# A two-layer relational graph network: 46 groups of edges of the second layer take their rows from on-chip memory instead of gathering them

## The chip, the cores and the metric

The kernel runs on one core of a Trainium2 chip. A core has five engines with queues of their own, each worked off in order: PE (TensorE, matrix products, with the weight loads counted apart as PEld), DVE (VectorE), ACT (ScalarE), POOL (GpSimd, which here issues the indirect gathers) and SP (SyncE, which here issues plain transfers). Engines wait for one another by semaphores. The metric is device time in microseconds of one execution; the kernel before took 4645.08 us (median of three runs, 4639.48 to 4657.33).

## The reference

There are 12500 nodes with 128 features each, 200000 edges sorted by target node, and 8 relations; source and relation of an edge are random. Each of two layers computes, for every node, the sum over relations of the mean of the messages that arrive by that relation, plus a root product and a bias; then a ReLU and the layer's input are added. At the end comes a layer norm over the features of the input plus the second layer's output.

```
W      = einsum('rb,bio->rio', comp, basis)
xw     = einsum('ni,rio->nro', x, W)
msgs   = xw[src, et]
seg    = dst * N_REL + et
summed = segment_sum(msgs, seg)
cnt    = segment_sum(ones, seg)
mean   = summed / maximum(cnt, 1)
agg    = mean.reshape(N_NODES, N_REL, HIDDEN).sum(axis=1)
h_new  = relu(agg + x @ root + bias);   h = h_new + h
...
out    = layernorm(x + h)
```

## The kernel before

Edges are cut into 1563 tiles of 128, and eight tiles form an octet (Q = 8, NQ = 196 octets; an octet has 1024 edges, the targets of which are some 64 neighbouring nodes). Targets are worked up in blocks of 128 nodes (98 of them), so an octet adds to one block, or to two.

Layer 1 gathers one row of x per edge, sums by node and relation with one-hot products (L1215), multiplies by the relation weights (L1247) and places the result in the block (L1278). As each block of its result is finished, `table` (L1346) multiplies it with all eight relation weights and writes the products to `y_d`, a table in HBM with a row for each pair of node and relation. The layer's result stays on chip as `hT`, features down the partitions and nodes along the columns.

Layer 2 gathers one finished row of `y_d` per edge (L678), so it has no relation products left. For octet q, the main loop puts into the queues: the gathers of octet q + 5; `slot_sums(q)`, eight products of 32 slots each that sum the gathered rows by target (L1442), and ACT's copy of the result `ys` (L628); `place_sums(q - 1)`, which puts the slots of the octet before at their nodes in the block's accumulator (L1467), with the root product where a block opens (L1471); the one-hot matrices of octet q + 2 on DVE (`slot_hots`: eight of 128x32 at L1091, one of 128x256 at L1094); and every second octet the closing of a block (L1299, L1303, L1323) and `open_block`, an ACT copy of a block of `hT`. After eight blocks a norm follows, with transposes on PE (L1585) and L1593 to L1613 on DVE. At its end an octet has `keep_on` (L1483): 12 products of 128x384 whose result nobody reads.

The rows of gathers lie in a ring of seven octet tiles; the gather of octet q + 7 waits until PE has read that of octet q. PSUM is used as fixed banks: `s` (two, the block accumulators in layer 2), `pt`, `ct`, `y` and two `po`; the slot sums of all octets and the norm's transposes share one `po`.

The order of work is written out by hand: each call appends to a list per engine, and `plan` turns the list into queues with semaphore waits. `plan.mark` names points at which an engine signals; with `plan.lazy` a wait is rounded up to the next such point.

In the list of functions below, the layer-1 loop and the layer-2 loop stand one after another; `later` is a list of small checks, of which one is done per octet.

Of the kernel before, what the change touches and what calls it, by code (L numbers as in the profile page):

```python
# [429 lines left out]
def ordered_path(  # L430
# [60 lines left out]
    BURST = 12  # L491
    DONE = NT - 4
    FULL = NQ - 4
    assert D == P and R * K == P and B == BF + 1 and 1 < TL and LAST < P and BF % 4 == 0 and Q == G and N % 2 == 0
    assert FULL == NQ - 4
# [61 lines left out]

    comp_sb = keep([P, L * R * NB], F32, "comp_sb")
# [38 lines left out]
    fails = keep([P, B + 4], F32, "fails")  # L597
# [54 lines left out]
    def gather(l, q):  # L652
        if q >= NQ:
            return
# [410 lines left out]
    def check_all():  # L1065
        pt, pc = pt_b
        pb = pt.rearrange("p b t -> p (b t)")
        pe(lambda: nc.tensor.matmul(pb[0:1, :B + 4], ones, fails, start=True, stop=True),
           ["ones"] + [("fails", b) for b in range(B + 4)], [pc])
        vec(lambda: nc.vector.tensor_reduce(nb_f, pb[0:1, :B + 4], axis=AX.X, op=ALU.max), [pc], ["nb_f"])  # L1070
        vec(lambda: nc.vector.tensor_copy(bad, nb_f), ["nb_f"], ["bad"])
# [27 lines left out]
    def onehot(l, q, g=None):  # L1099

        if l == 1 and q < FULL:
# [7 lines left out]
        if q >= NQ and (g is None or g < 0):  # L1109
            return  # L1110
# [264 lines left out]

    sT_all = [t.rearrange("p r g k -> p (r g k)") for t in sT_r.tiles]
    yr_all = [t.rearrange("p r d -> p (r d)") for t in yr_r.tiles]
    homes = {"idx": idx.bitcast(F32), "kr": kr, "sT0": sT_all[0], "sT1": sT_all[1], "yr0": yr_all[0], "yr1": yr_all[1],
# [14 lines left out]

    dm2_t = [home("sT0", Q * 2 * K, "dm2", i) for i in range(3)]
# [6 lines left out]
    dms2 = {}  # L1401
    hb_b = [(t, ("hb", i)) for i, t in enumerate((id_k, id_r, jmp.bitcast(F32)))]
    old.update({("hb", i): ["id_k", "id_r", "jmp"] for i in range(3)})
# [9 lines left out]
    hb = {}  # L1413
    misc = po_b[1]

    def open_block(k):
        n = rows_of(k)
        t, c = hb_b[k % 3]
        copy(t[:, :n], hT[:, k * P:k * P + n], [("h", k)], new(c))
        plan.mark("ACT")  # L1420
        hb[k] = t, c

# [10 lines left out]

    def slot_sums(q):
        t, c = rows_g.pop((1, q))
        d, dc = dms2.pop(q)
        b, bc = misc
        m0 = b[:, 3, :]

        def emit():  # L1440
            for i in range(Q):
                last = nc.tensor.matmul(m0[i // 2 * 2 * K:(i // 2 + 1) * 2 * K, :], d[:, i, :], t[:, i, :],  # L1442
                                        start=i % 2 == 0, stop=i % 2 == 1)
            return last

        pe(emit, [c + (0,), c + (1,), dc], [bc, ("done", 1)])
        plan.mark("PE")
        o, oc = ys[q] = ys_r.take()
        copy(o, m0, [bc], [oc])
        plan.mark("ACT")  # L1450

    def place_sums(q, k, opens, last):
# [5 lines left out]
        m = P  # L1458
# [17 lines left out]

    def keep_on():
        f = y_full[0]
        rhs = id_h[:, None, :].to_broadcast([P, 3, P])

        def emit():
            for _ in range(BURST):
                last = nc.tensor.matmul(f[:, :3, :], id_h, rhs, start=True, stop=True)  # L1483
            return last

        pe(emit, ["id_h"], [y_full[1]])
# [200 lines left out]
    def checks():  # L1687
        weights(1, (pt_b, pt_b))
        yield
        for b in range(B):  # L1690
            yield from check_edges(b)
        yield from check_span()
        yield from check_place()
        yield from fix_list()

# [19 lines left out]
    def end():  # L1715
        for k, step in ending:
            step()
            if k >= 0:
                tables.extend(table(k))
        ending.clear()  # L1720
# [8 lines left out]
    for o in range(NG - 3):  # L1729
# [11 lines left out]
        if parts is None:  # L1741
            run(later, 1)
# [22 lines left out]
        for i in range(2):  # L1765
            if turned_to:
                here = pt_b
                a, b = turned_to.pop(0)
            elif tables and o >= TABLE and (i == 0 or len(tables) > 6 or o > NG - 16):
                here = (pt_b, ct_b)[i]  # L1770
                a, b = tables.pop(0)(here)
            else:
                break
            while copies and here is not ct_b:
                copies.pop(0)(vcopy)
            a()
            if b is not None:
                copies.append(b)
        plan.mark("PE")
# [66 lines left out]
    for q in range(2):  # L1846
        onehot(1, q)
    open_block(0)
# [4 lines left out]
    for q in range(NQ):  # L1853
# [26 lines left out]
        if q == 0:  # L1880
            check_all()
        late = q - 1
        if q < FULL:
# [33 lines left out]
        if q < FULL:  # L1917
            keep_on()
# [67 lines left out]
```

## Time and profile before

| | |
|---|---|
| median of three runs | 4645.08 us (4639.48 to 4657.33) |
| profiled execution | 4616.74 us, span 4614.8 us |
| PE busy | 2424.3 us, 53% (weight loads 1713.5 us beside it) |
| DVE busy | 1386.0 us, 30% |
| ACT busy | 465.8 us, 10% |
| POOL busy | 2953.5 us, 64%, of which 1476.4 us in layer 1's gathers and 1475.0 us in layer 2's |
| mean granted clock of PE | 0.723 |
| DMA | 284.99 MB, mean 62 GB/s |

The profiled execution is 0.6% under the median of the runs. A row of the list of groups gives line, engine, operation, output and input, the count, the busy time and the mean of one in ns, and behind the bar the time in which the engine stood idle just before them, with what ended it. "issue" means that nothing the profile shows was waited for, "remote" that the releaser isn't in the records. Matrix products in float32 appear as two rows each, so eight of them are x16. The share of busy time is a mean over both layers; the prediction looks at layer 2 by itself, which lies between 2300 and 4600 us.

### The profile page before, as it was taken

To read this page: it belongs to the slowest core of one execution; us is meant where nothing else is said; L and a number is where in the kernel's file an instruction comes from. 1 tells how busy PE (TensorE), PEld (TensorE's weight loads), DVE (VectorE), ACT (ScalarE), POOL (GpSimd) and SP (SyncE) were. 2 spreads that over 40 slices of the span, in tenths; PEclk is the share of its full clock that TensorE was granted. 3 is DMA by queue.
4 is the path that set the end of the run, shared out by engine and by line. 5 is a ranking of instruction groups with operands and counts; after the bars stand their busy time and mean duration, and the time that the engine had idled before them with its cause. 6 is when DMAs were issued, how large, how long until landed. Compare 5 with 4: busy or idle time off the path is not lost.

```text
span 4614.8 us, 38428 instructions
## 1 busy us (share of the span) xinstructions
PE 2424.3 (53%) x14055; PEld 1713.5 (37%) x14055; DVE 1386.0 (30%) x4891; ACT 465.8 (10%) x1141; POOL 2953.5 (64%) x3135
## 2 busy tenths in 40 slices
PE   2666666555666566666644444444444444444445
PEld 1555554444555455555521222222222222222223
DVE  2544333333333233233312222222222222222223
ACT  0111112121211111111200000000000000000000
POOL 5666666666666666666556666666666666666664
PEclk9878777878777777777866666666666666666667
DMA  3111122223222222222221111112211212122121
GB/s 100 45 50 46 45 63 86 86 90 93 86 69 73 73 70 73 63 74 68 74 74 45 46 55 47 55 46 56 56 46 55 55 47 56 46 55 55 47 55 45
DMA packets 129830, 284.99 MB, mean 62 GB/s; under 512 B 54019, under 2 KB 61773, under 8 KB 129637
## 3 DMA queue, kind: packets, MB, share of 16 engines
q0 software_dynamic: 100064, 205.13, 17.1%
q10 hardware_dynamic: 16971, 52.05, 2.9%
q1 hardware_dynamic: 12602, 25.31, 1.6%
q8 instruction: 112, 1.84, 0.2%
q14 instruction: 81, 0.66, 0.0%
HBM read 223.63 MB, written 58.65 MB: 61 GB/s over the span
## 4 chain that ended last, share of the span: by engine, by line
another core or an unknown queue 41%; PE 32%; issue 20%; ACT 5%; DVE 2%; POOL 0%; DMA 0%; SPq 0%; ACTq 0%; POOLq 0%; DVEq 0%
PE y L1247 8%; PE y L1483 7%; PE s L1215 5%; PE po L1442 3%; ACT sT L628 2%; PE s L1467 2%; PE pt L1346 2%; PE po L1278 1%; ACT ys L628 1%; ACT y_row L628 1%; PE ct L1346 1%; DVE dm L1122 1%; PE po L1280 0%; PE s L1471 0%
## 5 line engine op out<-in xcount | busy, mean ns | idle before, releaser
L678 POOL DMA_INDIRECT rows<-in_x_dram,idx x1563 | 1476.4, 945 | 841.5 <-issue 438.7
L678 POOL DMA_INDIRECT rows<-y_d,idy x1563 | 1475.0, 944 | 768.9 <-issue 447.6
L1247 PE MATMUL y<-w_sb,sT 128*128 128x128 f32 x3136 | 544.9, 345 | 533.3 <-ACT ys L628 236.4
L1483 PE MATMUL y<-id_h 128*128 128x384 f16 x2304 | 598.3, 398 | 342.9 <-issue 335.2
L1247 PEld LDWEIGHTS y<-w_sb,sT 128*128 128x128 f32 x3136 | 512.0, 255 | 558.1 <-ACT ys L628 245.2
L1122 DVE TENSOR_SCALAR dm<-cols,kr,w 128x128 f32<-128x128 f16 x1563 | 526.1, 402 | 493.4 <-remote 232.4
L1091 DVE TENSOR_SCALAR sT<-cols,kr,w 128x32 f32<-128x32 f16 x1536 | 352.8, 302 | 724.7 <-remote 543.4
L1442 PE MATMUL po<-rows,sT 128*32 128x128 f32 x3072 | 173.5, 354 | 712.1 <-ACT ys L628 437.4
L1215 PEld LDWEIGHTS s<-dm,rows 128*128 128x128 f32 x3126 | 434.5, 217 | 175.3 <-ACT sT L628 106.3
L1483 PEld LDWEIGHTS y<-id_h 128*128 128x128 f16 x2304 | 259.7, 114 | 643.2 <-issue 563.8
L1215 PE MATMUL s<-dm,rows 128*128 128x128 f32 x3126 | 451.2, 303 | 81.3 <-ACT sT L628 61.7
L1442 PEld LDWEIGHTS po<-rows,sT 128*32 128x32 f32 x3072 | 102.2, 136 | 799.8 <-ACT ys L628 463.5
L628 ACT ACTIVATE sT<-s 128x512 f32<-128x512 f32 x391 | 212.4, 596 | 804.5 <-remote 543.6
L628 ACT ACTIVATE ys<-po 128x128 f32<-128x128 f32 x192 | 53.2, 277 | 2111.9 <-remote 1871.6
L1299 DVE TENSOR_TENSOR po<-po,carry 128x128 f32<-128x128 f32 x98 | 29.2, 298 | 663.1 <-remote 406.8
L1299 DVE TENSOR_TENSOR s<-s,carry 128x128 f32<-128x128 f32 x97 | 28.9, 298 | 616.4 <-remote 387.7
L1346 PE MATMUL pt<-w_sb,arena 128*128 128x512 f32 x258 | 156.3, 678 | 48.5 <-issue 41.2
L1467 PE MATMUL s<-pl,ys 128*128 128x256 f32 x288 | 139.6, 572 | 14.3 <-issue 14.2
L1278 PE MATMUL po<-pl,ys 128*128 128x256 f32 x392 | 138.9, 438 | 15.1 <-DVE pl L1130 6.5
L628 ACT ACTIVATE y_row<-pt 128x512 f32<-128x512 f32 x131 | 78.4, 598 | 659.2 <-remote 451.3
L1585 PE MATMUL po<-ident,wide 128*128 128x128 f32 x96 | 23.5, 388 | 193.6 <-ACT ys L628 153.3
L871 PE MATMUL ct<-arena,id_h 128*128 128x512 f16 (+1 forms) x188 | 75.5, 422 | 85.9 <-issue 44.5
(214 smaller groups left out, 1565.0 us busy)
## 6 DMA issues: line engine op xcount, KB each, us to landing
y_d<-y_row ACTq DMA_DIRECT2D x96, 512.0 KB
rows<-in_x_dram,idx POOLq DMA_INDIRECT x1563
rows<-y_d,idy POOLq DMA_INDIRECT x1563
x_g<-in_x_dram SPq DMA_DIRECT2D x24, 512.0 KB
out_dram<-x_g SPq DMA_DIRECT2D x12, 512.0 KB
arena<-in_L_gnn_basis_dram SPq DMA_DIRECT2D x2, 512.0 KB
w_d<-y_row SPq DMA_DIRECT2D x2, 512.0 KB
w_sb<-w_d SPq DMA_DIRECT2D x2, 512.0 KB
```

The costliest lines, as they stand in the source:

```text
L628: act(lambda: nc.scalar.activation(out_t, in_t, AF.Copy), reads, writes)
L678: ins.append(nc.gpsimd.indirect_dma_start(out=t[:, i - q * Q, :], out_offset=None, in_=table_t, in_offset=bass.IndirectOffsetOnAxis(ap=ids ...
L871: nc.tensor.matmul(ct[:, :nb, :], id_h, eq[:, s - s0, :nb, main], start=(s == 1), stop=False)
L1091: vec(in_turn([lambda i=i: nc.vector.tensor_scalar(t[:, i, :], cols[:, :2 * K], kr[:, i0 + i:i0 + i + 1], w[:, i0 + i:i0 + i + 1], op0=ALU ...
L1122: emits.append(lambda i=i: nc.vector.tensor_scalar(t[:, i - q * Q, :wide], cols[:, :wide], ids[:, i:i + 1], w[:, i:i + 1], op0=ALU.is_equa ...
L1215: last = nc.tensor.matmul(s_b[i // 4][0][:, i % 4, :], t[:, i, :], d[:, i, :], start=True, stop=True)
L1247: last = nc.tensor.matmul(y[:m], t[:, r, :nt, :].rearrange("p t k -> p (t k)"), w_sb[:, 0, r, :], start=(r == 0), stop=(r == R - 1))
L1278: ins = nc.tensor.matmul(a, o[:m], t[:m], start=opens, stop=last and not root_in)
L1346: pe(lambda: nc.tensor.matmul(hb[:n].rearrange("p r d -> p (r d)"), hT[:, j * P:j * P + n], w_sb[:, 1, k * H:(k + 1) * H, :].rearrange("p ...
L1442: last = nc.tensor.matmul(m0[i // 2 * 2 * K:(i // 2 + 1) * 2 * K, :], d[:, i, :], t[:, i, :], start=i % 2 == 0, stop=i % 2 == 1)
L1467: ins = nc.tensor.matmul(a, o[:m], t[:m], start=opens, stop=last and not root_in and not fixed)
L1483: last = nc.tensor.matmul(f[:, :3, :], id_h, rhs, start=True, stop=True)
```

## The change

46 of the 196 octets, every fourth from the ninth on (`ROUTED`), take no gathers in layer 2. 368 of its 1563 gathers and the slot sums of these octets go. Their messages are formed from `hT` instead.

In layer 1, `hT` is turned block by block once it is no longer needed as it is (`turn_rows`, four transposes and a copy for four blocks), so that nodes lie down the partitions. For each routed octet a list is made of where its edges go: source nodes are split into groups of 256, an edge has a rank among the edges of its half octet (512 edges) and group, and 32 ranks are kept for each group. `values` prepares this; `groups_of`, `earlier_of`, `ranks_of` and `slots_of` do it for one octet in each of the layer-1 octets 96 to 142 (DVE, four products and eight small ones on PE, two ACT copies), and three SP stores put it into HBM (`lo_d`: the source within the group by slot, `sc_d`: target and relation, and the weight's reciprocal). During these octets the tables have one bank instead of two. Two more checks guard the lists (at most 40 target nodes in half an octet, at most 32 edges in a slot group); if one is violated, the kernel's general path computes the result, as with the checks that it had.

In layer 2, a routed octet is done in seven steps, six of four units and one of two small ones, spread 2, 2, 2, 1 over four octets. A unit has 128 slots. `compare` (DVE) makes one-hot matrices of slot against node within the group, two of 128x512 per step; `pick_rows` (PE) multiplies them with `hT`, 32 products of 32x128 per step into the one bank `pt`, and ACT copies the result; `slots_in` (DVE) makes the matrix of slot against relation and node, 128x320, weighted, one per unit; `add_up` (PE) multiplies the picked rows with it, one product of 128x320 per unit, summing over a half octet in the banks `y` and `po`; `relate` multiplies the two sums with the eight relation weights, and its copy is the octet's `ys`, from which `place_sums` goes on as before. In one loop step t the queues get compare(t + 1), pick_rows(t), slots_in(t - 1), add_up(t - 2). Two SP loads per routed octet bring the list back, one of them spread to all partitions.

Since `hT` is turned, `open_block` now transposes on PE before its copy. The slot sums of the other octets write the bank `ct` instead of `po`. `keep_on` is gone; its bank now serves `add_up`.

What PE has in its queue in layer 2 before, toward the end of the full octets; `y<-id_h` is `keep_on`, `rows_105` a ring tile of gathered rows:

```order
L1442 MATMUL po_139<-rows_109,sT_112 32x128 x8
L1467 MATMUL s_136<-iota_f,ys_120 128x256
L1471 MATMUL s_136<-jmp,w_sb 128x128
L1483 MATMUL y<-id_h 128x384 x12
L1442 MATMUL po_139<-rows_110,sT_112 32x128 x8
L1467 MATMUL s_136<-pl_114,ys_117 128x256
L1483 MATMUL y<-id_h 128x384 x12
```

The same engine in the changed kernel, in the same part; `dm` holds the one-hot matrices, `arena` is `hT`, `pt` the picked rows:

```order
L1745 MATMUL po_139<-ident,dm 128x52
L1765 MATMUL pt<-arena,dm 32x128 x32
L1787 MATMUL po_138<-arena,idx 128x320 x4
L1873 MATMUL ct<-rows_107,sT_112 32x128 x8
L1898 MATMUL s_136<-pl_114,ys_120 128x256
L1765 MATMUL pt<-arena,dm 32x128 x32
L1787 MATMUL po_138<-arena,sT_113 128x320 x4
L1676 MATMUL po_139<-ident,arena 128x128
L1765 MATMUL pt<-arena,dm 32x128 x32
L1787 MATMUL y<-arena,sT_113 128x320 x4
L1873 MATMUL ct<-rows_108,sT_112 32x128 x8
L1898 MATMUL s_135<-pl_115,ys_118 128x256
```

Between the slot sums of one gathered octet and the next now stand two steps of the routed one (L1765 picks, L1787 sums up), in the place of the 12 products nobody read.

DVE in the same part before; `wide` and `carry` belong to the closing of a block:

```order
L1091 TENSOR_SCALAR sT_112<-cols,kr,w 128x32 x8
L1094 TENSOR_SCALAR iota_f<-cols,pos 128x256
L1299 TENSOR_TENSOR s_136<-s_136,carry_122 128x128
L1303 TENSOR_SCALAR carry_121<-s_136,bias_t 128x128
L1091 TENSOR_SCALAR sT_112<-cols,kr,w 128x32 x8
L1094 TENSOR_SCALAR pl_114<-cols,pos 128x256
```

And DVE in the changed kernel; `dm<-arena` is a comparison and `arena<-y_row` the matrix of slots:

```order
L1715 TENSOR_SCALAR dm<-arena,pair 128x512 x2
L1734 TENSOR_SCALAR arena<-y_row_127,comp_sb 128x320 x4
L1715 TENSOR_SCALAR dm<-arena,pair 128x512 x2
L1734 TENSOR_SCALAR arena<-y_row_127,sel 128x320 x4
L1146 TENSOR_SCALAR sT_112<-cols,kr,w 128x32 x8
L1149 TENSOR_SCALAR iota_f<-cols,pos 128x256
L2020 BN_STATS st_133<-x_g_128 128x6 x8
L1361 TENSOR_TENSOR s_136<-s_136,carry_122 128x128
L1365 TENSOR_SCALAR carry_121<-s_136,bias_t 128x128
```

Each step adds six DVE operations ahead of the one-hots of a gathered octet (L1146, L1149), which are unchanged.

The diff, cut to what the prediction speaks of:

```diff
-    BURST = 12
...
+    BT = 4
+    CAP = 32
+    NW = 40
+    GU = P // CAP
+    NGH = -(-NT // 2)
+    NTL = -(-NGH // GU)
...
+    TU = 4
+    SEG = R * NW
...
+    EVERY = 4
+    ROUTED = list(range(FROM + 10 * EVERY // NU + 2, 192, EVERY))
...
     def gather(l, q):
-        if q >= NQ:
+        if q >= NQ or l == 1 and q in ROUTED:
             return
...
+    def compare(t):
...
+        vec(in_turn([lambda c=c: nc.vector.tensor_scalar(outs[c], a, node_p[:, c:c + 1], None, op0=ALU.is_equal)
+                     for c in range(2)]), [bc, "node"], new(oc))
+        plan.mark("DVE")
...
+    def slots_in(t):
...
+            vec(lambda o=o, n=n, x=x: nc.vector.tensor_scalar(
+                o[:n], segs[:n], sg[:n, x:x + 1], sg[:n, BR * NTL + x:BR * NTL + x + 1], op0=ALU.is_equal,
+                op1=ALU.mult), [segs_b[1], sgc], new(oc))
+        plan.mark("DVE")
...
+    def pick_rows(t):
...
+                        last = nc.tensor.matmul(b[k * CAP:(k + 1) * CAP, x, :], o[:n, c * HC + at:c * HC + at + CAP],
+                                                hT[:n, j * P:(j + 1) * P], start=c == 0, stop=c == 1)
...
+        copy(g[:m, :n * P], b[:m, :n, :].rearrange("p t d -> p (t d)"), [bc], new(gc))
+        plan.mark("ACT")
...
+    def add_up(t):
...
+                last = nc.tensor.matmul(seg_b[b][0].rearrange("p t d -> p (t d)")[:, :SEG], g[:n, x * P:(x + 1) * P],
+                                        o[:n], start=z in (0, NTL), stop=z in (NTL - 1, BR * NTL - 1))
...
+    def route_step(t):
+
+        i, u = t // NU, t % NU
+        if u == 0 and i < NR:
+            unit_rows(i)
+        compare(t + 1)
+        if i < NR:
+            pick_rows(t)
+        if 0 <= t - 1 < NR * NU:
+            slots_in(t - 1)
+        if 0 <= t - 2 < NR * NU:
+            add_up(t - 2)
+        if u == 3 and i >= 1 and i - 1 < NR:
+            relate(i - 1)
+        if u == 1:
+            fetch_rows(i + 1)
+        if u == NU - 1:
+            fetch(i + 2)
...
     def slot_sums(q):
...
-        b, bc = misc
+        b, bc = ct_b
...
-    def keep_on():
-        f = y_full[0]
-        rhs = id_h[:, None, :].to_broadcast([P, 3, P])
...
+        route(q, 0)
         late = q - 1
-        if q < FULL:
+        if q < FULL and q not in ROUTED:
             slot_sums(q)
         if 0 <= late < FULL:
             place_sums(late, sup(late), *opened_by(late))
         if q >= FULL:
             add_rows(q, k, opens, last)
+        route(q, 1)
         onehot(1, q + 2)
         if sup(q + 2) != sup(q + 1) and q + 2 < NQ:
             open_block(sup(q + 2))
+        route(q, 2)
...
-        if q < FULL:
-            keep_on()
```

More of the change, by code (lines that the diff above doesn't have):

```diff
@@ L594, in ordered_path @@
     y_b.append((ct_b[0][:, 0, :], ct_b[1]))
-    fails = keep([P, B + 4], F32, "fails")
+    fails = keep([P, B + 6], F32, "fails")
     fix = keep([P, 3], F32, "fix")
@@ L1099, in onehot @@
     def onehot(l, q, g=None):
-        if l == 1 and q < FULL:
+        if l == 1 and q < FULL and q not in ROUTED:
             slot_hots(q)
@@ L1109, in onehot @@
         if q >= NQ and (g is None or g < 0):
+            return
+        if l == 1 and q in ROUTED:
+            i = ROUTED.index(q)
+            o, c = pl[q] = pl2_r.take()
+            vec(lambda: nc.vector.tensor_scalar(o[:2 * NW], cols[:2 * NW], pos2[:2 * NW, i:i + 1], None,
+                                                op0=ALU.is_equal), ["cols", "pos2"], new(c))
+            plan.mark("DVE")
             return
@@ new lines, in ordered_path, with relate @@
+    for i in range(2):
+        for k in range(BR):
+            old[sum_b[i][1] + (k,)] = old[sum_b[i][1]]
+    def relate(i):
+        t_s, sc = sum_b[i % 2]
+        t4 = t_s.rearrange("p (r b n) -> p r b n", r=R, b=BR)
+        b, bc = misc
+        pe(in_turn([lambda r=r: nc.tensor.matmul(
+            b[:BR * NW, 0, :], t4[:, r].rearrange("p b n -> p (b n)"), w_sb[:, 1, r, :], start=r == 0, stop=r == R - 1)
+            for r in range(R)]), [sc + (k,) for k in range(BR)] + [("w", 1, r) for r in range(R)], [bc])
+        plan.mark("PE")
+        o, c = ys[ROUTED[i]] = ys_r.take()
+        copy(o[:BR * NW], b[:BR * NW, 0, :], [bc], [c])
+        plan.mark("ACT")
@@ L1423, in slot_numbers, with route @@
+    for t in range(NR * NU + 5):
+        steps_of.setdefault(FROM + t * EVERY // NU, []).append(t)
+    def route(q, n):
+        for t in steps_of.get(q, [])[n:n + 1 if n < 2 else None]:
+            route_step(t)
     def slot_numbers():
@@ L1432, in slot_numbers, with begin_routes @@
         plan.mark("DVE")
+    def begin_routes():
+        vec(lambda: nc.vector.tensor_copy(segs[:, :2 * P], cols), ["cols"], new(segs_b[1]))
+        vec(lambda: nc.vector.tensor_scalar(segs[:, 2 * P:], cols[:, :SEG - 2 * P], float(2 * P), None, op0=ALU.add),
+            ["cols"], [segs_b[1]])
+        fetch_rows(0)
+        for i in range(2):
+            fetch(i)
     def slot_sums(q):
@@ L1694, in checks @@
         yield from fix_list()
+        yield from values()
     later = checks()
@@ L1741, in ordered_path @@
         if parts is None:
-            run(later, 1)
+            run(later, 5 if o < SORT - 2 else 1)
+        if 0 <= o - SORT - 1 < NR:
+            ranks_of(o - SORT - 1)
+        if 0 <= o - SORT < NR:
+            groups_of(o - SORT)
+        plan.mark("DVE")
         if not opened:
```

330 lines of the change are left out of this document (318 added, 12 removed).

## The prediction

> **What bounds the kernel now.** I read the page's list of groups first, then busy times by stretch, then the waits of layer 2, and last the timeline in two places. In the stretches the columns are length, busy time of PE, PEld, DVE, ACT and POOL with counts, granted clock, DMA share and GB/s.
>
> ```profile
> L678 POOL DMA_INDIRECT rows<-y_d,idy x1563 | 1475.0, 944 | 768.9 <-issue 447.6
> ...
> 1000.00:2000.00 1000.00, 624.71 (x3341) 522.87 (x3339) 320.94 (x1024) 172.03 (x370) 655.06 (x694) 0.77 0.26 76
> 2600.00:4400.00 1800.00, 787.12 (x4988) 407.57 (x4985) 464.18 (x1924) 62.75 (x248) 1188.07 (x1259) 0.66 0.19 52
> ...
> ACT ys L628 <- remote: 1550.9, 99, 20.3
> POOL rows L678 <- issue: 356.2, 1166, 0.5
> POOL rows L678 <- remote: 249.6, 87, 4.6
> ```
>
> In layer 2 (2600 to 4400) 1259 gathers take 1800 us, 1.43 us each: 11.4 us an octet, 45.8 us for four. A gather is busy 0.944 us, and 356.2 us over 1166 gaps is 0.31 us more before the next, so 1.25 us is the pitch while POOL runs; the other 0.18 us is the 249.6 us in which POOL stands, 87 times, for the ring of row tiles. PE is busy 44%, DVE 26%. So gathers fill 87% of the time, yet POOL does wait for PE, and ACT's copy of the slot sums waits 1551 us on something that the profile can't name. The timeline shows when that happens:
>
> ```profile
> 2638.07 0.66 PE L1442 MATMUL po<-rows,sT 128*32 128x128 f32 x16
> 2638.66 0.70 PE L1467 MATMUL s<-iota_f,ys 128*128 128x256 f32 x2
> 2639.20 0.38 PE L1471 MATMUL s<-id_k,w_sb 128*128 128x128 f32 x2
> 2640.37 0.94 POOL L678 DMA_INDIRECT rows<-y_d,idy  x1 [0.30 <-issue]
> ...
> 2650.35 0.94 POOL L678 DMA_INDIRECT rows<-y_d,idy  x1 [0.30 <-issue]
> 2654.27 0.28 ACT L628 ACTIVATE ys<-po 128x128 f32<-128x128 f32 x1 [18.65 <-remote]
> 2654.51 0.94 POOL L678 DMA_INDIRECT rows<-y_d,idy  x1 [3.22 <-remote]
> 2654.60 1.12 PE L1585 MATMUL po<-ident,wide 128*128 128x128 f32 x4 [15.02 <-ACT ys L628]
> ```
>
> PE issued the slot sums at 2638.07 and what follows by 2639.6. ACT got the result at 2654.27, 16 us later, after gathers had run end to end and POOL had stood still for 3.2 us. Here is the opposite case, with POOL idle:
>
> ```profile
> 4515.46 0.94 POOL L678 DMA_INDIRECT rows<-y_d,idy  x1 [0.30 <-issue]
> ...
> 4519.69 1.10 PE L1442 MATMUL po<-rows,sT 128*32 128x128 f32 x16 [11.26 <-ACT ys L628]
> 4520.72 1.22 PE L1467 MATMUL s<-iota_f,ys 128*128 128x256 f32 x2
> 4521.73 0.64 PE L1471 MATMUL s<-id_r,w_sb 128*128 128x128 f32 x2
> 4522.16 2.60 PE L1483 MATMUL y<-id_h 128*128 128x384 f16 x12
> ...
> 4527.87 0.66 PE L1442 MATMUL po<-rows,sT 128*32 128x128 f32 x16
> 4528.63 0.28 ACT L628 ACTIVATE ys<-po 128x128 f32<-128x128 f32 x1 [2.70 <-PE po L1442]
> 4529.22 2.11 PE L1483 MATMUL y<-id_h 128*128 128x384 f16 x12
> 4531.26 0.66 PE L1442 MATMUL po<-rows,sT 128*32 128x128 f32 x16
> 4532.26 0.94 POOL L678 DMA_INDIRECT rows<-y_d,idy  x1 [15.85 <-PE po L1442]
> ...
> 4553.53 0.28 ACT L628 ACTIVATE ys<-po 128x128 f32<-128x128 f32 x1 [17.48 <-issue]
> ```
>
> Without gathers ACT follows PE by 0.76 us (4527.87 to 4528.63) and an octet takes 3.4 us; soon after they resume, a copy waits 17.5 us again. So two things bound layer 2: POOL's pitch, and PE's results arriving late while POOL gathers. Why they do is not in the profile.
>
> **The change, step by step.** I count for four octets of layer 2, one of them without gathers, 46 times; now 45.8 us.
>
> POOL: 8 of 32 gathers go. 24 × 1.25 = 30.0 us, or 34.3 at 1.43.
>
> DVE, from these rows:
>
> ```profile
> L1091 DVE TENSOR_SCALAR sT<-cols,kr,w 128x32 f32<-128x32 f16 x1264 | 290.3, 302 | 595.5 <-remote 454.2 <-PE po L1442 85.3 <-issue 20.6
> L1094 DVE TENSOR_SCALAR pl<-cols,pos 128x256 f32<-128x256 f16 x118 | 56.0, 475 | 0.0
> L1593 DVE TENSOR_TENSOR x_g<-po,x_g 128x512 f32<-128x512 f32 x20 | 13.8, 692 | 214.7 <-PE po L1585 138.0 <-remote 76.7
> ...
> 4529.42 1.84 DVE L1091 TENSOR_SCALAR sT<-cols,kr,w 128x32 f32<-128x32 f16 x8 [0.38 <-PE s L1471]
> ```
>
> Eight 128x32 take 1.84 us, 0.23 each; 128x256 takes 0.475. That is 1.1 ns per column, so 128x320 should take 0.55 and 128x512 0.76 (estimates from these two). The comparisons: 12 × 0.76 and two small ones, 9.7 us. The one-hots of slots: 26 × 0.55 = 14.2. Gone are 1.84 us of one octet; the three other octets keep 3 × 2.3 = 6.9. Closing two blocks, the norm, and rows of the units: 4.5. Sum 35.
>
> PE, with full clock: eight slot sums start 0.59 us ahead of the next operation (2638.07 to 2638.66), 0.074 each; 196 picks of the same form, 14.5 us. One 128x256 of L1467 takes 0.54 to the next start. A 128x320 is between that and 0.68 (by columns): 26 make 14.0 to 17.6. The eight products with the weights, each half of a 128x256: 2.2. Three octets of their own, 3 × (0.59 + 0.54) = 3.4; roots and transposes, which now serve to open a block too, 2. Sum 36 to 40, I take 38. Removed are 4 × 2.11 us of filler products (L1483); they stood where PE waited and are worth nothing. At half clock the same rows read 1.03 (4519.69 to 4520.72) and 1.01 (4520.72 to 4521.73), so PE would need about 70.
>
> ACT: eight copies of 512 or 320 columns and a few small ones, under 8 us by the row below; SP: two loads, the larger of which lands 0.85 MB, asked for a whole group ahead, which at 62 GB/s (the row's mean) is 14 us of 46; both hidden.
>
> ```profile
> DMA packets 129830, 284.99 MB, mean 62 GB/s; under 512 B 54019, under 2 KB 61773, under 8 KB 129637
> ...
> L628 ACT ACTIVATE sT<-s 128x512 f32<-128x512 f32 x391 | 212.4, 596 | 804.5 <-remote 543.6
> ```
>
> PE and DVE don't simply overlap. Each pick needs a comparison and the one bank it writes, which ACT must have copied (0.6 us and two handovers); each sum needs the copy and the slots. With three buffers each, this runs near the longer of the two, 40 us at full clock, but every group puts seven PE-to-ACT results one after another where there were four.
>
> What clock? 0.66 is granted at 44% busy PE, 0.77 at 62% (the stretches above). PE would be nearer to the second row: 38/0.77 = 49 us. More density would raise the clock; results that arrive late under the remaining 24 gathers lower it, and I let these two cancel. Late results are bounded by 0.8 us (POOL idle) and 16 (the burst), seven or so per group. Layer 1, where PE does 62% of its time in useful work under the same gathers, says that dense work is not stopped for 16 us each time. I take 49.
>
> Layer 1 additions: turning h (25 × four transposes and a copy) and the slot lists of 46 octets: some 2.5 us DVE, 2 us PE, 1 us ACT per octet. There DVE is busy 3.7 of 11.5 us and PE 7.2, so most is hidden under POOL; but the tables lose one of two banks meanwhile. Bounds 0 (idle time covers it) and 46 × 1 us; I take 10.
>
> Sum: 46 × (49 − 45.8) = 147, plus 10, on the profiled execution's 4616.7: 4774. The median of the runs is 28 above it (4645.1), so 4802.
>
> **Rivals.**
> *B, faster: PE stays at full clock and late results only follow dense gathers.* Then 40 us a group: 46 × −5.8 = −267, plus 10: 4388. POOL alone, at 34.3, would give −529 and 4126. For it: POOL has room to run ahead, since a group holds 8 us without gathers, and the case at 4519 shows the whole chain moving at 3.4 us an octet then. Against: that case is rare, and layer 1 never reaches full clock. It decides once PE's share falls under 45.8 us, a mean clock of 0.83. The Trainium skill, TensorE: Matmul & The Clock Gate, Part 1, has just two clocks, full after about 3.4 us of steady work and half after an idle window; by it a PE with 38 of 40 us of work would stay at full. The trace agrees on both values (12 fillers in 2.11 against 2.60 us), not on how long they last here.
>
> *C, much slower: every handover of the chain pays what the burst shows.* If three more results per group wait 4 to 5 us, 60 to 65 us: 46 × 16 = 736, 5390 at most; PE at half clock gives 70 and 5770. For it: 99 waits averaging 15.7 us in the row above. Against: layer 1.
>
> *D, POOL is slowed by DVE.* DVE's busy time in a group goes from 12 to 35 us. If the 24 us of new work kept POOL out whenever they met, a gather's 0.944 us would grow: 30 + 24 = 54 us a group, 46 × 8 = 368 and about 5020. The rows speak against it: gathers take 944 ns in layer 2 with DVE at 26%, and the 1.1 ns per column shows no doubled reading. The Trainium skill, SBUF — State Buffer, Who interferes with whom, says that a tensor_scalar in a two-port mode locks GpSimd out for the whole instruction; no row here shows that.
>
> *E, the second path.* Two new checks (more than 39 nodes in half an octet, more than 31 edges in a slot group) could send the kernel through its general path, whose time no row shows. Half an octet holds 512 edges and 16 edges per node, about 33 nodes. Negligible.
>
> **How the numbers follow.** My forecast A (49 us a group, a range of 46.5 to 53 or 4690 to 4990) has 0.38, B 0.38, C 0.17, D 0.05, others 0.02. The likeliest time 4800 is A's. The overall range takes in most of B, to 38.5 us a group (4320), and C up to 58 us (5220); POOL alone and half clock lie outside, together 0.15. About 0.5% is what can be told from no change. Faster are B and a little of A: 0.40; same is A's lower edge, 0.04; slower the rest, 0.56.
>
> **What would show it.** In the changed profile: 1195 gathers on y_d instead of 1563, still 0.94 us; layer 2's groups of four octets at 49 us with PE over 75% busy at a clock near 0.77, DVE about 75%; POOL waiting on PE for 10 us or more a group. B is right if POOL's standing time stays under 10 us a group and the clock is over 0.9; C if ACT's copies of picks wait over 5 us on average; D if the mean gather exceeds 1 us. I am wrong above all if PE's clock is not what layer 1 has, or results arrive late in another measure than there.

## The result, and the profile after

The changed kernel takes 5268.24 us (median of four runs, 5260.76 to 5276.94), the kernel before 4649.89 us beside it: a ratio of 1.1332, 95% interval 1.1299 to 1.1366. It is 13% slower, where 4800 us was forecast and 4320 to 5220 given as the range.

The page of the changed kernel, its list of groups and its busy times by stretch (length, busy time of PE, PEld, DVE, ACT and POOL with counts, clock, DMA share, GB/s), then its waits between 2600 and 4400 us:

```profile
span 5259.8 us, 78732 instructions
...
L733 POOL DMA_INDIRECT rows<-y_d,idy x1195 | 1193.2, 999 | 1671.1 <-PE ct L1873 1333.8
...
L1765 PE MATMUL pt<-arena,dm 128*32 128x128 f32 (+1 forms) x18032 | 968.3, 303 | 531.6 <-issue 273.6
...
1000.00:2000.00 1000.00, 633.94 (x3829) 526.57 (x3828) 428.69 (x1127) 192.35 (x458) 651.99 (x683) 0.78 0.27 74
2600.00:4400.00 1800.00, 1411.02 (x16034) 972.43 (x16033) 760.86 (x2536) 188.04 (x467) 738.17 (x736) 0.87 0.16 47
...
POOL rows L733 <- PE ct L1873: 874.2, 92, 18.1
```

1195 gathers are left on `y_d`, as the change says. 736 of them take 1800 us in layer 2, so the 24 of a group of four octets take 58.7 us, where the four octets took 45.8. That is 46 x 12.9 = 593 us; with the 33 us that layer 1 loses (below) 626, against 618 measured. POOL now stands still for 874 of these 1800 us, and always for PE's slot sums; PE is busy 78%. So PE bounds layer 2. Layer 1 costs a little as well. The first gather of layer 2 starts 33 us later (after, then before):

```profile
2355.34 0.94 POOL L733 DMA_INDIRECT rows<-y_d,idy  x1 [9.27 <-DMA y_d<-y_row]
```

```profile
2322.38 0.94 POOL L678 DMA_INDIRECT rows<-y_d,idy  x1 [2.24 <-issue]
```

Now PE within one group of the changed kernel. First its own rows around one resumption of the gathers, then POOL's in the same stretch (3600 to 3613 us):

```profile
3602.81 2.30 PE L1765 MATMUL pt<-arena,dm 128*32 128x128 f32 x53
3605.34 0.49 PE L1765 MATMUL pt<-arena,dm 128*32 128x128 f32 x4 [0.23 <-issue]
3606.81 0.49 PE L1765 MATMUL pt<-arena,dm 128*32 128x128 f32 x3 [0.98 <-issue]
3608.27 0.60 PE L1765 MATMUL pt<-arena,dm 128*32 128x128 f32 x4 [0.97 <-issue]
3609.72 2.50 PE L1787 MATMUL po<-arena,sT 128*128 128x320 f32 x8 [0.85 <-issue]
...
3602.58 0.94 POOL L733 DMA_INDIRECT rows<-y_d,idy  x1 [14.20 <-PE ct L1873]
...
3611.32 0.94 POOL L733 DMA_INDIRECT rows<-y_d,idy  x1 [0.30 <-issue]
3614.18 0.60 ACT L683 ACTIVATE idx<-pt 128x512 f32<-128x512 f32 x1 [11.56 <-PE po L1676]
```

and the same step at 4009 us, with POOL standing still since before and until 4014.78:

```profile
4009.47 2.02 PE L1765 MATMUL pt<-arena,dm 128*32 128x128 f32 x64
...
4014.78 0.94 POOL L733 DMA_INDIRECT rows<-y_d,idy  x1 [14.81 <-PE ct L1873]
```

With POOL idle, the 64 rows of a pick step start within 1.75 us at full clock (3.25 at half), and the next operation follows at once. With gathers running, 53 rows go off as fast; then they come in threes and fours every 1.46 us, though no semaphore stands between them ("issue"), and ACT's copy of the step comes at 3614.18, 3 us after the last gather was issued and 5 us after the last pick. Over the 244 full steps between 2600 and 5000 us the trace's records give a mean of 3.92 us from first to last start: 2.30 for the 121 steps with no gather beside them, 5.5 for the 123 others.

The rows inside a step are only one of two delays; the result of the step is late as well. Of the 183 full steps up to 4400 us, 91 have no gather beside them or before their copy, and ACT's copy starts 0.37 us after the last pick has started. In the 92 others, three of the six full steps of a group, it starts 4.45 us after. All steps write the one bank `pt`, so PE waits for these copies. The picks' row between 2600 and 4400 us has, behind the bar, PE's idle time before them and what ended it, and below is the row of most of the copies:

```profile
L1765 PE MATMUL pt<-arena,dm 128*32 128x128 f32 x11836 | 627.6, 303 | 328.2 <-issue 154.5 <-ACT sT L683 103.8 <-ACT idx L683 55.4
...
L683 ACT ACTIVATE sT<-pt 128x512 f32<-128x512 f32 x123 | 73.5, 597 | 825.0 <-remote 366.4 <-PE pt L1765 319.8 <-PE po L1676 127.2
```

PE stands 159 of 1800 us for ACT's copies, 5.2 us a group, and 155 us, 5.0 a group, between picks with nothing that it waits for.

### The profile page after: what moved, and what is told of

Same layout as the page of the kernel before. It is cut to its first block, busy times and chain, and to the rows that moved or that the text cites. A ratio compares the mean times of both kernels' runs of the same rounds, so it can differ in the third digit from the quotient of the medians.

```text
span 5259.8 us, 78732 instructions
## 1 busy us (share of the span) xinstructions
PE 3652.3 (69%) x32975; PEld 2715.0 (52%) x32975; DVE 2149.4 (41%) x6759; ACT 710.4 (14%) x1673; POOL 2680.6 (51%) x2767
## 4 chain that ended last, share of the span: by engine, by line
PE 47%; another core or an unknown queue 36%; issue 9%; ACT 6%; DVE 2%; DMA 0%; ACTq 0%; DVEq 0%
PE pt L1765 13%; PE po L1787 7%; PE y L1309 6%; PE y L1787 6%; ACT sT L683 3%; PE s L1277 3%; PE ct L1873 2%; PE po L1811 2%; PE s L1898 1%; PE pt L1408 1%; ACT y_row L683 1%; PE po L1340 1%; ACT ys L683 1%; PE ct L1408 1%
## 5 line engine op out<-in xcount | busy, mean ns | idle before, releaser
L733 POOL DMA_INDIRECT rows<-y_d,idy x1195 | 1193.2, 999 | 1671.1 <-PE ct L1873 1333.8
L1765 PE MATMUL pt<-arena,dm 128*32 128x128 f32 (+1 forms) x18032 | 968.3, 303 | 531.6 <-issue 273.6
L1765 PEld LDWEIGHTS pt<-arena,dm 128*32 128x32 f32 (+1 forms) x18032 | 704.0, 119 | 771.9 <-issue 459.5
L1734 DVE TENSOR_SCALAR arena<-y_row,comp_sb 128x320 f32<-128x320 f16 (+1 forms) x598 | 233.1, 445 | 618.6 <-PE y L1787 332.3
L1734 DVE TENSOR_SCALAR arena<-y_row,sel 128x320 f32<-128x320 f16 (+1 forms) x598 | 231.5, 442 | 616.0 <-remote 240.9
L1787 PE MATMUL po<-arena,sT 128*128 128x320 f32 (+1 forms) x798 | 305.6, 526 | 9.0 <-issue 8.1
L1787 PE MATMUL y<-arena,sT 128*128 128x320 f32 x798 | 273.3, 484 | 1.2 <-issue 1.0
L1146 DVE TENSOR_SCALAR sT<-cols,kr,w 128x32 f32<-128x32 f16 x1168 | 268.2, 303 | 2.5 <-PE s L1902 2.4
L1715 DVE TENSOR_SCALAR dm<-arena,pair 128x512 f32<-128x512 f16 (+1 forms) x644 | 257.5, 442 | 11.3 <-remote 8.0
L1787 PEld LDWEIGHTS po<-arena,sT 128*128 128x128 f32 (+1 forms) x798 | 174.4, 229 | 112.3 <-issue 75.7
L1787 PEld LDWEIGHTS y<-arena,sT 128*128 128x128 f32 x798 | 154.6, 206 | 83.9 <-issue 39.5
L1787 PE MATMUL po<-arena,idx 128*128 128x320 f32 (+1 forms) x398 | 149.5, 520 | 4.2 <-issue 4.0
```

Source lines behind the costliest of these rows:

```text
L733: ins.append(nc.gpsimd.indirect_dma_start(out=t[:, i - q * Q, :], out_offset=None, in_=table_t, in_offset=bass.IndirectOffsetOnAxis(ap=ids ...
L1146: vec(in_turn([lambda i=i: nc.vector.tensor_scalar(t[:, i, :], cols[:, :2 * K], kr[:, i0 + i:i0 + i + 1], w[:, i0 + i:i0 + i + 1], op0=ALU ...
L1715: vec(in_turn([lambda c=c: nc.vector.tensor_scalar(outs[c], a, node_p[:, c:c + 1], None, op0=ALU.is_equal) for c in range(2)]), [bc, "node ...
L1734: vec(lambda o=o, n=n, x=x: nc.vector.tensor_scalar(o[:n], segs[:n], sg[:n, x:x + 1], sg[:n, BR * NTL + x:BR * NTL + x + 1], op0=ALU.is_equal,
L1765: last = nc.tensor.matmul(b[k * CAP:(k + 1) * CAP, x, :], o[:n, c * HC + at:c * HC + at + CAP], hT[:n, j * P:(j + 1) * P], start=c == 0, s ...
L1787: last = nc.tensor.matmul(seg_b[b][0].rearrange("p t d -> p (t d)")[:, :SEG], g[:n, x * P:(x + 1) * P], o[:n], start=z in (0, NTL), stop=z ...
```

## The experiments

**Is it a limit on PE's instructions?** The picks bring 784 products and weight loads per group, and in the kernel before the octets had about 5.5 of these per us. Theory T was that PE gets no more than that under gathers. Two kernels change the instruction count of the kernel before. In this section a time without an interval is that of a single run.

```diff
-        if q < FULL:
-            keep_on()
```

> The kernel before without its filler products, nothing else. Theory T (while gathers run, PE gets through only some 5.5 matrix instructions and weight loads per us, whatever their size): an octet of layer 2 has 40 of them instead of 64, PE is no longer what POOL waits for, and the octet goes from 11.4 us toward POOL's own 10.0: up to -270 us, ratio about 0.95. Rival F (the filler holds the clock up and costs nothing, as the prediction had it): the clock of layer 2 falls from 0.66 toward 0.5, the time stays within 1% or rises.

Measured: 4619.23 us against 4645.15, ratio 0.9939 (0.9922 to 0.9956). The clock of layer 2 fell to 0.53, as rival F had it, but the pace did not change with 24 fewer instructions per octet; the 26 us gained are far from the 270 of T.

```diff
-    BURST = 12
+    BURST = 36
...
-        rhs = id_h[:, None, :].to_broadcast([P, 3, P])
+        rhs = id_h
...
-                last = nc.tensor.matmul(f[:, :3, :], id_h, rhs, start=True, stop=True)
+                last = nc.tensor.matmul(f[:, 0, :], id_h, rhs, start=True, stop=True)
```

> The kernel before with 36 filler products of 128 columns in place of 12 of 384: the same columns and nearly the same array time, three times the instructions. Theory T (a limit on PE's instructions per us under gathers): an octet has 112 instructions instead of 64, 15 to 20 us instead of 11.4, so 700 us or more slower. Rival (PE's array time or the clock counts): within 2% of before.

Measured: 4710.15 us, 1.4% over 4645.15, a tenth of what T asked for. T falls: the count of instructions does not set the pace of the kernel before. How PE is held in it shows better without the filler. This is the timeline of the kernel without it:

```profile
2985.70 1.10 PE L1442 MATMUL po<-rows,sT 128*32 128x128 f32 x16 [3.96 <-issue]
2986.74 1.22 PE L1467 MATMUL s<-pl,ys 128*128 128x256 f32 x2
...
3005.48 0.94 POOL L678 DMA_INDIRECT rows<-y_d,idy  x1 [0.30 <-issue]
3010.68 0.28 ACT L628 ACTIVATE ys<-po 128x128 f32<-128x128 f32 x1 [25.03 <-remote]
3010.92 0.94 POOL L678 DMA_INDIRECT rows<-y_d,idy  x1 [4.49 <-remote]
```

PE has almost nothing to do, and still its slot sums of 2985.70 reach ACT at 3010.68, when the gathers have stopped for 4.3 us.

**Is it the gathers at all?** In the next kernel the gathers of layer 2 are left out (all but the first octets and the last twelve), so it sums whatever lies in the ring.

```diff
         rows_g[l, q] = (t, cell)
+        if l == 1 and Q <= q < NQ - 12:
+            return
```

> The changed kernel with the gathers of layer 2 left out but for the first octets and the last twelve; everything else runs on whatever the ring holds. Theory T (gathers hold PE up): no pick burst over 3.3 us, a group of four octets falls from 58 us to 43 or less, total about 4550. Rival P (PE's own work is simply longer than was estimated): the group stays over 54 us, total over 5080.

Measured: 4224.87 us. The stretch of layer 2:

```profile
2600.00:4100.00 1500.00, 1468.62 (x21608) 1092.20 (x21606) 1020.75 (x3439) 260.23 (x627) 31.15 (x32) 0.99 0.10 34
```

PE is busy 98% at a clock of 0.99. The changed kernel has 16034 PE rows in 30.7 groups, 523 a group; here 21608 rows, 41.3 groups, come in 1500 us: 36.3 us a group. Every full step of picks up to 4000 us takes 1.75 us. So PE's own work is 36 us, and the gathers add 22. Rival P is out. T's group of "43 or less" holds, but its total of about 4550 was 325 us too high.

**Their traffic, or POOL's way of issuing them?** Here one plain load of SP brings as many rows of the same size from the same table, neighbouring ones instead of those wanted.

```diff
         rows_g[l, q] = (t, cell)
+        if l == 1 and Q <= q < NQ - 12:
+            load(t, y_d[q * Q * P // 2:q * Q * P // 2 + Q * P, :].rearrange("(i p) d -> p i d", p=P), y_done,
+                 [cell + (0,), cell + (1,)])
+            return
```

> The changed kernel with each octet's gathers of layer 2 replaced by one plain load of SP that brings as many rows of the same 512 bytes from the same table, neighbouring rows in place of the wanted ones (but for the first and the last octets). If it is the traffic of the gathers into on-chip memory that holds PE, picks still take over 5 us and the total stays over 5000. If it is POOL's way of issuing them, a group falls to 36 to 40 us as it did without gathers, total 4230 to 4400.

Measured: 4233.47 us, the same as with none:

```profile
2600.00:4100.00 1500.00, 1465.78 (x21673) 1091.50 (x21665) 1021.21 (x3443) 262.22 (x631) 31.17 (x32) 0.99 0.27 77
```

77 GB/s, more than the 47 of the changed kernel, and no effect on PE. Here too every full step up to 4000 us takes 1.75 us. It is not the bytes that arrive; it is how POOL issues them, or their being scattered, which this run does not tell apart. For the issuing speaks a run with drains below: there 930 gathers of scattered rows in 1800 us hold PE less than the 736 of the changed kernel do.

**Does the picks' size matter?** Picks in float16 on a constant matrix, so the picked rows are not those wanted:

```diff
-                        last = nc.tensor.matmul(b[k * CAP:(k + 1) * CAP, x, :], o[:n, c * HC + at:c * HC + at + CAP],
-                                                hT[:n, j * P:(j + 1) * P], start=c == 0, stop=c == 1)
+                        last = nc.tensor.matmul(b[k * CAP:(k + 1) * CAP, x, :], o.bitcast(F16)[:n, c * HC + at:c * HC + at + CAP],
+                                                id_h[:n], start=c == 0, stop=c == 1)
```

> The changed kernel with its picks as float16 products on a constant matrix, so the picked rows are not those wanted: half of the picks' instructions and a quarter of their array time. Theory T: 392 of some 1040 instructions of a group go, most of them issued under gathers; the group falls from 58 to about 42 us, total about 4530. Rival P: what goes is array time at the clock granted, 9 to 12 us of a group, total about 4750 to 4850.

Measured: 4605.4 us, 13% less than the changed kernel. In its stretch of 1500 us there are 800 gathers, so a group takes 45 us. That lies between the two, nearer to T, which had fallen by then. The picks had less work as well as fewer instructions, so the time alone does not tell which of the two counts. The trace tells a little more: between 2600 and 4400 us the rows of a step, 32 here, start within 0.53 us on average with no gather beside them and 1.13 with gathers, but ACT's copy still starts 4.35 us after the last pick with gathers, against 0.32. Shorter picks shrink the hold within a step, and the results stay late.

**A queue that PE stands behind?** In the kernel before, POOL's pauses are longest after the longest runs of gathers (on average 3.1 us after 8, 2.8 after 16, 4.6 after 24). Theory Q: gathers are issued faster than something behind POOL works them off. The next kernels slow POOL down by a drain.

```diff
                 for i in range(i0, i1):
                     ins.append(nc.gpsimd.indirect_dma_start(
...
+                    if l == 1:
+                        nc.gpsimd.drain()
```

> The kernel before with a drain of POOL behind every gather of layer 2, which stretches POOL's own pitch from 1.25 us by some tenths. Theory Q (gathers at 1.25 us fill a queue that empties at some 1.43 us each, and PE's results stand behind that queue until POOL pauses): at a pitch of 1.4 to 1.5 us the queue stays short, ACT's copies of the slot sums follow PE within 2 us, and the time stays within 3% of before. Rival V (PE is held while a gather is being issued, whatever the pitch): the waits of ACT stay at 11 us and more, and every tenth of us costs 1563 x 0.1 = 156 us.

> The changed kernel with the same drain behind every gather of layer 2. Theory Q: picks take 1.75 to 3.3 us as they do with POOL idle, a group of four octets falls from 58 us to about 40, total about 4450. Rival V: POOL's part of a group gets longer and PE is held for longer, total 5300 or more.

Measured: 7546.97 us (ratio 1.6245, 1.6218 to 1.6272) and 6549.74 us. Q missed both times, because a drain is far dearer than the tenths I had put: the pitch is 3.3 us. V's signs were met to the letter (over 5300; ACT's copies wait 26 us on average), but not for V's reason: at that pitch POOL bounds everything (24 gathers 84 us), and the waits are for rows to land. PE tells what was asked. First the kernel before with drains:

```profile
3002.16 1.11 PE L1444 MATMUL po<-rows,sT 128*32 128x128 f32 x16 [21.49 <-DMA rows<-y_d,idy]
...
3003.34 0.28 ACT L628 ACTIVATE ys<-po 128x128 f32<-128x128 f32 x1 [24.62 <-PE po L1444]
```

In it ACT's copies start 0.49 us on average after the last row of the slot sums has started (0.58 at most, 2600 to 5000 us), as Q had it ("within 2 us"); in the kernel before it is 8.92 us (2600 to 4400 us). Then the changed kernel with drains:

```profile
4002.91 0.95 POOL L733 DMA_INDIRECT rows<-y_d,idy  x1 [2.31 <-issue]
...
4004.77 2.02 PE L1767 MATMUL pt<-arena,dm 128*32 128x128 f32 x64
...
4006.25 0.95 POOL L733 DMA_INDIRECT rows<-y_d,idy  x1 [2.40 <-issue]
4006.72 2.42 PE L1789 MATMUL y<-arena,idx 128*128 128x320 f32 x8
```

64 rows go off in 2.02 us with gathers on both sides, as they do with POOL idle. In all of layer 2 the steps take 2.23 us in the mean, and never over 3.24, half clock. So PE is not held by the issuing of a gather alone (V is out), but when gathers follow one another without a drain or a pause between them.

> The changed kernel with a memset of 48 columns and a drain behind every gather of layer 2, a still wider pitch. Theory Q: as with the drain alone, or better if that one did not reach 1.43 us; with a pitch over 1.7 us, 24 gathers bound the group at over 41 us, total about 4500. Rival V: slower than with the drain alone, total over 5300.

```diff
+                    if l == 1:
+                        nc.gpsimd.memset(pace, 0.0)
+                        nc.gpsimd.drain()
```

Measured: 6530.79 us, as with the drain alone: the memset fits into the time that the drain takes anyway.

**How many gathers does it take?** Drains behind every second, fourth and eighth gather.

```diff
+                    if l == 1 and (i - i0) % 4 == 3:
+                        nc.gpsimd.drain()
```

> The changed kernel with a drain of POOL behind every second gather of layer 2. A drain adds 2.07 us (3.32 less 1.25, the pitches measured with and without). Theory H (PE runs freely for the first two or three gathers after POOL has emptied its work and is held from then until it has emptied it again): PE is not held, POOL bounds the group at 24 x 1.25 + 12 x 2.07 = 55 us, total about 5090, picks at 1.75 to 3.3 us. Rival R (PE's rate falls in proportion to the gathers per us): picks in between, some 2.5 us under gathers, total 5090 as well.

> A drain behind every fourth gather: POOL needs 30 + 6 x 2.07 = 42.4 us a group. Theory H: PE is held for the last one or two gathers of four, 1 to 3 us six times a group, 36 us of work and 6 to 18 us: group 42 to 50, total 4500 to 4860. Rival R: gathers per us as in the changed kernel's bursts less a third, PE at half speed under them: group about 55, total 5090.

> A drain behind every octet's eight gathers: POOL needs 30 + 3 x 2.07 = 36.2 us a group. Theory H: PE is held for some 7 us of each burst of 10, 36 + 21 = 57 us, total about 5190, little better than without drains. Rival (any regular pause sets PE free): group about 42, total 4500.

Measured: 5253.12, 4646.49 and 5198.26 us. The stretches of layer 2, for 2, 4 and 8:

```profile
2600.00:4400.00 1800.00, 1294.71 (x16226) 938.82 (x16224) 779.80 (x2583) 196.67 (x472) 728.01 (x739) 0.84 0.16 47
```

```profile
2600.00:4400.00 1800.00, 1613.82 (x20105) 1148.00 (x20105) 965.83 (x3216) 239.40 (x586) 951.41 (x930) 0.96 0.21 59
```

```profile
2600.00:4400.00 1800.00, 1390.07 (x15957) 963.89 (x15958) 760.06 (x2537) 187.83 (x465) 733.29 (x733) 0.87 0.16 47
```

| drain behind every | pick step, mean us | group, us (24 x 1800 / gathers) | bound by |
|---|---|---|---|
| gather | 2.23 | 84 | POOL |
| second | 2.27 | 58.5 | POOL |
| fourth | 3.22 | 46.5 | POOL and PE alike |
| eighth | 3.57 | 58.9 | PE |
| none | 3.92 | 58.7 | PE |

Adding drains, which only cost POOL time, makes the kernel 12% faster at four, and this as H has it: two in a row leave PE nearly free, four hold it in part, eight nearly as much as none. Rival R (in proportion to gathers per us) would have had 5090 at two and four alike. The rival at eight (any regular pause sets PE free, 4500) is out as well. H's 5090 at two was 160 us too low because a drain after two gathers adds 2.3 us on average rather than 2.07 (2.4 after four), and the gathers themselves average 0.99 us there. One gap remains: at eight, H's 5190 is right to 0.2%, but that was close to the time without drains anyway.

> The kernel before with a drain behind every octet's eight gathers. POOL needs 8 x 1.25 + 2.07 = 12.1 us an octet where the octet takes 11.4 now. Theory H: POOL emptied its work in its pauses before as well, so the drain takes their place for the most part: 0.7 us x 184 octets = 130 us slower, ratio about 1.03; ACT's copies wait at most one burst, 10 us. Rival: the drain comes on top of the pauses, 2.07 x 184 = 380 us slower.

Measured: 4796.23 us, against 4603.84 of the kernel before beside it: 192 us slower, nearer to H's 130 than to 380. 1153 gathers in 1800 us are 12.5 us an octet, which is POOL's own time; ACT's copies wait up to 13.3 us where H had 10; they start 0.49 us after the slot sums, and PE now waits 994 of the 1800 us for rows to land:

```profile
PE po L1444 <- DMA rows<-y_d,idy: 994.1, 144, 8.6
```

So by this one run the drains took the place of a part of the pauses, as H had it, and PE's results came at once; yet no time was to be won by it there, since POOL's own time then bounds the kernel.

None of these makes the change pay: with drains at four it comes to 4646 us, 0.9% over the kernel before beside it (one run each). Of the kernels that still fetch the rows that are wanted, the only one that beats both is the kernel before without its filler, by 0.6%.

## Why the prediction was wrong

- **The bounds named were right, their weight was not.** POOL's pitch and "PE's results arriving late while POOL gathers" both showed. The price of the second is 22 us a group (58.7 less 36.3), more than all that the change could win.
- **POOL's term** (24 x 1.25 = 30 us) held within 5%: gathers now average 999 ns instead of 944, which makes 31.3 us.
- **DVE's term** was too high: 760.86 us in 30.7 groups is 24.8 us, not 35. A comparison (128x512) takes 0.43 us of busy time, not 0.76, and a one-hot of slots (128x320) 0.39, not 0.55. Scaling by columns was wrong for both, in two ways. The figures it started from are of different kinds: 0.23 is the time from one 128x32 to the next, and 0.475 the duration of a single 128x256; a single 128x32 lasts 0.302. And both rows read `cols`, which the kernel keeps in PSUM, while comparisons and slot matrices read tiles in SBUF. By their durations 512 columns of the one take no longer than 256 of the other (changed kernel, 2600 to 4400 us):

```profile
L1715 DVE TENSOR_SCALAR dm<-arena,pair 128x512 f32<-128x512 f16 x366 | 158.1, 474 | 0.0
...
L1149 DVE TENSOR_SCALAR pl<-cols,pos 128x256 f32<-128x256 f16 x60 | 28.7, 479 | 0.0
```

That the place of the input makes the difference is not tested by a run. The term bounds nothing.
- **PE's term** was right: 36 to 40 us at full clock was the estimate, 36.3 us is the group without gathers.
- **The step that failed** is the one from 38 to 49 us: "More density would raise the clock; results that arrive late under the remaining 24 gathers lower it, and I let these two cancel." The clock did rise, to 0.87, which alone would give 38/0.87 = 44 us. But late results don't act through the clock alone; they cost time of their own, which the sum put at nothing, though the prediction bounded it by 0.8 to 16 us for each of some seven results. In three of the six full steps of a group the copy came 4.45 us after the last pick instead of 0.37, and PE stood 5.2 us a group for such copies. On top of that comes what the prediction did not have at all: once a few gathers follow one another, PE's own issue is held, in the example three or four rows each 1.46 us, and these steps take 5.5 us instead of 2.30. The sum needed a term of its own for them, and had none. The two overlap with other work and with the lower clock (0.87 against 0.99 without gathers), so what share of the 22 us each has is not known.
- **The support taken from layer 1 was misread.** That PE is busy 62% there under gathers was read as "dense work is not stopped". But a held PE reads as busy: in the changed kernel's layer 2 it shows 78% busy, 46 us of a group, for work that takes 36. The forecast's sign "PE over 75% busy" thus came true by luck. How much of layer 1's 62% is held is open; no run leaves its gathers out.
- **The removed filler** was priced at nothing; leaving it out of the kernel before gains 0.6%, so that step was near enough.
- **Layer 1** cost 33 us, not 10; the bounds given (0 to 46) held it.
- **Rival C** came closest: 60 to 65 us a group and 5390 "at most", with a chance of 0.17. Its mechanism showed in part. It had three more results per group that wait 4 to 5 us, and that is what the copies of picks do (three steps of six, 4.45 us). But not every handover pays, and the hold within a step, where there is no handover, was not in it. Its sign (ACT's copies of picks wait over 5 us on average) is met by ACT's idle time before them, 825.0 us over 123 copies or 6.7 us, though most of that is time in which the picks were not yet done: the lateness alone is 2.42 us over all full steps. What spoke against C, layer 1, was the misread support. Its "at most" was also added up wrongly: 65 us a group makes 4645 + 10 + 46 x 19.2 = 5538, and 5390 stands for 62. **Rival B** was ruled by a condition it named itself, PE's share under 45.8 us at a mean clock of 0.83. The clock was 0.87 and B still did not come, since the condition left out the hold. The Trainium skill's rule beside B (TensorE: Matmul & The Clock Gate, Part 1: full clock under steady work) agrees where PE runs unheld: 0.99 without gathers. The prediction's 2.11 and 2.60 us for twelve fillers are not the two clocks, being 1.23 apart; the full steps' 1.75 and 3.25 us come nearer, and the granted clock in the records is 0.5 or 1.0 and nothing between.
- **Rival D** showed in small. The row of the changed kernel:

```profile
3741.57 1.26 POOL L733 DMA_INDIRECT rows<-y_d,idy  x1 [0.30 <-issue]
3741.84 0.87 DVE L1715 TENSOR_SCALAR dm<-arena,pair 128x512 f32<-128x512 f16 x2
```

A gather beside a comparison takes 1.26 us, here and on average over 176 such gathers; the 175 that have a slot matrix (L1734) alone beside them average 1.00. Of the 844 in layer 2 with neither beside them none takes over 1.05 us, of the 351 others 167. In the whole kernel 190 of 2758 gathers take over 1.05 us and lose 76 us together, against 8 and 1.5 us in the kernel before. D's sign, a mean gather over 1 us, stands on the edge with 0.999. The price per column that spoke against D came from rows that read `cols`, in PSUM; the comparisons and slot matrices read SBUF. The Trainium skill (SBUF — State Buffer, Who interferes with whom) says that such DVE instructions can lock GpSimd out; that fits. POOL stands 874 of 1800 us for PE, so it should cost little here; no run tests that.
- **The range** missed by 48 us. Its upper end stopped at 58 us a group, inside C, whose own figures went on to 65.

What is not settled: what it is in POOL's issuing that holds PE. It is not the bytes, not a single gather, and not the count of PE's instructions in the kernel before; it builds up over two to four gathers in a row and is gone after a drain or a pause of POOL. That instructions are loaded late is an unlikely cause: between 2600 and 4100 us the packets of 16 KB of the queue of kind "instruction" take 1.12 us in the changed kernel and 1.06 without gathers, and one comes every 14 us, while PE is held every 1.46 us in the example. Scattered rows from another engine than POOL were not tried.

## What to carry to other kernels

Work that is moved from an engine that looks like the bound to another one costs what it costs beside what is left on the first: before pricing it from a quiet stretch, look for the same operation in a busy one, and give an unexplained wait a term of its own with both its ends. A busy share does not tell whether an engine works or is held; its work without the neighbour does, and leaving the neighbour out is one run. Where gathers run end to end beside an engine that bounds the kernel, a pause after every few can be worth more than it costs (12% here with drains at four); where the gathers themselves are the bound it is not (the kernel before lost 192 us with drains at eight).

## What was not expected of the hardware

- Indirect gathers issued end to end at 1.25 us hold PE's issue after the first few (in the example to three or four rows per 1.46 us) and make its results late; pick steps then take 5.5 us instead of 2.30 in the same kernel (1.75 at full clock), and ACT's copy comes 4.45 us after the last pick instead of 0.37. Plain loads at 77 GB/s do nothing of the kind.
- A drain of POOL behind a gather adds 2.1 to 2.5 us, though the gather's own row is 0.94 us long. Whether this is work of the gather that comes after its row, or the drain's own price, no run tells apart.
- A 128x512 comparison from float16 in SBUF to float32 took 0.474 us, no longer than a 128x256 one-hot (0.479 us, L1149) with its input in PSUM.
- A gather's own row grew from 0.944 to 1.26 us on average beside such comparisons, and stayed at 0.944 with neither a comparison nor a slot matrix beside it.
